# Row totals of the attention scores: accumulating DMAs in DRAM and a block transpose instead of products with a matrix of ones, for 21 of 32 graphs

## The chip, the core and the metric

The kernel runs on one core of one Trainium2 chip, in one launch. The metric is device time in microseconds (us); lower is better. A time is the median of several executions of the same program. Beside it stands one execution that was taken by the hardware profiler; all durations of single instructions come from that one.

The engines are called by their short names: PE is the matmul engine (PEld is its loading of weights), DVE the vector engine, ACT the scalar engine, POOL is GpSimd, SP the engine that issues most of the DMAs.

## What is computed

The input is `x`, 32 graphs of 512 nodes with 128 features each, and one 512 x 512 adjacency matrix `adj`. Four graph layers follow each other, each as `x = x + layer(relu(layernorm(x)))`. The change is in the first one:

```python
x_h = elu(x @ Wi + bi)
a_src = x_h @ We[:H, 0]
a_tgt = x_h @ We[H:, 0]
e = sigmoid(a_tgt[:, :, None] + a_src[:, None, :] + be[0])
e = e * (adj + ALPHA * (1.0 - (adj != 0)))
agg = einsum('bij,bjh->bih', e, x_h)
self_part = x_h * sum(e, axis=-1, keepdims=True)
recv = elu(concatenate([agg, self_part], -1) @ Wn + bn)
out = concatenate([recv, x_h], -1) @ Wm + bm
```

For each graph the scores `e` are a 512 x 512 matrix, and `self_part` needs the total of each of its 512 rows: these are the "score totals". Layer 2 (`layer1` in the code) is a gated recurrence of five steps with products by `adj`, layer 3 one product with `adj`, layer 4 a polynomial in `adj`.

## The kernel before, in words

**Layout.** Features (or source nodes) lie on the 128 partitions. One graph is a tile of 128 x 512 fp32 (256 KB), so nearly every instruction works on 128 x 512 elements. Scores are kept transposed, as four tiles `es[0..3]` (lines 701 to 710), one for each 128 source nodes, with all 512 target nodes along the free dimension. A total over the source nodes is therefore a sum over the four tiles and over the 128 partitions.

**The order of the work.** The kernel doesn't issue its instructions where they are written. Each step is listed with `op(engine, us, due, ...)`: an engine, an assumed duration, a due time, and what it reads and writes. A planner (`Plan`, lines 53 to 248) plays the program through with these assumed durations, and puts the steps of each engine in a fixed order. `slots` (line 301) gives the number of buffers of each kind, `ahead` how far it may look past the oldest step; `HEAD_NUDGES` (line 25) are seeds that shift some due times in the first 130 us of the plan. On the chip each engine runs its list in order, and waits by semaphores where a result is late. So a step that waits holds up everything that stands behind it on its engine, and for a DMA everything behind it in the queue of the engine that issues it. While nothing is ready for PE in the first 50 us of the plan, it issues small products of `ones` that nothing reads (`plan.idle`, line 347), here called fillers.

**A branch.** After some 11 us the kernel knows whether `adj` holds only zeros and ones (lines 586 to 596, 1106), and takes one of two arms. With these inputs it takes the binary one. In it, `adj` products run on PE in a one-pass format (fp32r), with the other operand split into a rounded part and a rest.

**Pipelining over graphs.** Graphs enter one after the other, some 50 us apart (`PACE`, `begin`, line 774), and several are in different layers at the same time. For a graph, `entry` and `scored` (line 625) make `xhT`, the messages `msg` and the score ends; `aggregated` (line 694) makes the scores, their products with the messages (line 715, bank `pn`), the totals, and the rest of the layer.

**The totals before.** For graphs 0 and 1 two DVE additions and two products with `ones`. For graph 2 three DVE additions, and for graphs 3 to 31 DMAs, add the four `es` tiles to one tile `sums` in SBUF: a copy issued by SP (line 740), then three accumulating DMAs issued by POOL (line 743), each of which waits for the one before it. The sum over the partitions is left to PE: ACT rounds `sums` to fp32r (line 747), DVE takes the rest (line 748), and two products with `ones_r` (line 753) add them up in a bank `ps`, where each total then stands on all partitions. DVE multiplies it with `xhT` (`own`, line 756), and the product of `own` with `Wn` is added to `pn` (line 758), which has stayed open until then.

**A column as a row.** `scored` already has a way to turn a column of four values per partition (the score ends) to a row on all partitions, without PE (lines 662 to 671): a DVE block transpose, a DMA to a small DRAM tile `d`, and a DMA that reads it back to all partitions.

**Layer norm.** Each layer norm (line 513) has DVE moments, a power on POOL (line 527) and a scaling on ACT (line 536). The powers share POOL's queue with the accumulating DMAs.

**Masks and loads at the start.** `adj` is loaded by ACT's queue (line 386), graphs and weights by SP's (lines 383 to 401). ACT copies `adj` to fp32r with its columns reordered (line 583, `nat`), copies its transpose (line 584, `adj_r`) and makes the four mask tiles (line 828). The products of line 906 make the square of `adj`.

Of the kernel before, what the change touches and what calls it, by code (L numbers as in the profile page):

```python
# [17 lines left out]
P = 128  # L18
# [6 lines left out]
HEAD_NUDGES = (7100000, 7100078, 7100153, 7100154, 7100740, 7100413, 7100768, 7100794, 7100559, 7100664, 7100595,  # L25
    7100631, 7100754, 7100963, 7100652, 7100659, 7100662, 7100678, 7100697, 7100699, 7100706,
    7100965, 7100730, 7100733, 7100742, 7100786, 7100966, 7100797, 7100813, 7100877, 7100824,
    7100834, 7100860, 7100864, 7100866, 7100875, 7100881, 7100884, 7100901, 7100907, 7100908,
    7100911, 7100919, 7100920, 7100922, 7100934, 7100936, 7100941, 7100945, 7100946, 7100949,
    7100950, 7100955, 7100970, 7100973)  # L30
# [22 lines left out]
class Plan:  # L53
# [74 lines left out]
    def known(self, o, to):  # L128

        own = {"PE": 0.0, "ACT": 0.13, "DVE": 0.13}  # L130
        if to.eng == o.eng in own:
            return o.known - o.result + own[o.eng]
        return o.known + (self.slack if to.eng == "PE" else 0.0)
# [118 lines left out]
def tile_four_graph_layers(  # L252
# [38 lines left out]
    FIRST = 4  # L291
    ONES = 0
    SPLIT = False
    SQUARE, NAT = 12.0, 0.0
    BRANCHES = 0.75
    A_LANDS = (3.0, 3.3, 3.6, 3.8)
# [4 lines left out]
    slots = {"x": 5, "f": 36, "q": 4, "s": 8, "d": 4, "m": 8, "b": 8}  # L301
    plan = Plan(slots, ahead=60.0, last=(B - 2) * PACE)
# [8 lines left out]
    def buffers(pool, kind, n, shape, dt=F32):  # L311
# [6 lines left out]
        "s": buffers(pool, "s", slots["s"], [P, 12 * NC]),  # L318
        "d": buffers(dram, "d", slots["d"], [P, 32]),
# [15 lines left out]

    def chunks(t):
        return t.rearrange("p (c d) -> p c d", c=NC)
# [4 lines left out]
    op("DVE", 0.2, -9, lambda: nc.vector.memset(at(ones), 1.0), [], [ones])  # L342
# [12 lines left out]
    op("ACT", 1.4, -9, lambda: nc.scalar.activation(  # L355
# [12 lines left out]
    def load_column(src, name, due, result=None):  # L368
        return load_const(src.rearrange("(p o) -> p o", o=1), [P, 1], name, due, 0.48, result=result)
# [7 lines left out]
    def load_graph(b, due, result=None):  # L377
        op("SP", 0.48, due, lambda: nc.sync.dma_start(
            at(X[b]), x[b].rearrange("(p c) d -> p c d", c=NC)),
            [], [X_group[b // G], X[b]] if b % G == 0 else [X[b]], result=result)  # L380


    load_graph(0, -10, 2.5)
    A_nat = [Val("f") for _ in range(NC)]
    for ic, v in enumerate(A_nat):
        load(v, adj.rearrange("(p c) n -> c p n", c=NC)[ic], -9.5, 0.45, result=A_LANDS[ic], eng="ACT")
    Wi_sb = load_const(Wi, [P, P], "Wi_sb", -9)
    bi_sb = load_column(bi, "bi_sb", -9)
    load_graph(1, -8.5, 4.3)
    load_graph(2, -8, 4.5)  # L390
# [3 lines left out]
    load(W_tok, Wn[:P], -7, to=lambda t: t[:, :P], result=4.5)  # L394
    load(W_tok, We.rearrange("(t p) o -> p (t o)", p=P), -7, to=lambda t: t[:, P:])
    be_sb = load_const(be.partition_broadcast(P), [P, 1], "be_sb", -7, result=4.3)
    Wn_sb = load_const(Wn[P:], [P, P], "Wn_sb", -6, result=4.0)
    bn_sb = load_column(bn, "bn_sb", -6, result=3.6)
    Wm_sb = load_const(Wm.rearrange("(t p) o -> p t o", p=P), [P, 2, P], "Wm_sb", -5)
    bm_bc = load_const(bm.partition_broadcast(P), [P, P], "bm_bc", -5, earliest=BRANCH)  # L400
    load_graph(3, -6, 3.6)
# [153 lines left out]
    plan.vals[mask] = True  # L555
# [22 lines left out]
    adj_r = const("adj_r", [P, NC, N], F32R)  # L578
    adj_rows = [Val(tile=adj_r.tile[:, jc, :]) for jc in range(NC)]
    plan.vals.update(dict.fromkeys([adj_r, *adj_rows]))  # L580
    nat = [Val("q") for _ in range(NC)]
    for jc, pt in enumerate(adjacency_turned(-1)):
        op("ACT", T_COPY, NAT + jc, lambda jc=jc: nc.scalar.copy(chunks(at(nat[jc])), by_token(A_nat[jc])), [A_nat[jc]], [nat[jc]])
        op("ACT", T_COPY, jc, lambda jc=jc, pt=pt: nc.scalar.copy(at(adj_rows[jc]), at(pt)),
           [pt], [adj_rows[jc], adj_r])
# [38 lines left out]

    def scored(b, hT, due):
# [33 lines left out]
        row, tgt = Val("d"), Val("f")  # L659

        flip = Val("s")
        def turn():
            nc.vector.transpose(
                at(flip)[:, :32].rearrange("p (k c) -> p k c", c=NC),
                at(ends)[:, None, NC : 2 * NC].to_broadcast([P, 32 // NC, NC]))
        def gather():
            nc.sync.dma_start(at(row), at(flip)[:, :32])
        def read():
            rows = at(row).rearrange("(q k) i -> q (k i)", k=32)[:, :P]
            nc.sync.dma_start(  # L670
                at(tgt).rearrange("p (q e) -> p q e", e=P), rows[None].to_broadcast([P, 4, P]))
# [12 lines left out]
        if b < G:  # L684
            tgt = Val("b")
            tgt.pieces = True
            op("PE", T_TR, d, spread, [ends, ident], [tgt])
        else:
            op("DVE", 0.1, d, turn, [ends], [flip])
            op("SP", T_DMA, d, gather, [flip], [row], result=2.6)  # L690
            op("SP", T_DMA, d, read, [row], [tgt], keep=KEEP, result=5.0)
        return xhT, msg, ends, tgt, like_tgt, of_tgt

    def aggregated(b, begun, due):
# [7 lines left out]
        for jc in range(NC):  # L702
# [5 lines left out]
                at(e), at(e), 1.0, at(mask)[:, jc, :], op0=ALU.add, op1=ALU.mult),  # L708
                [e, mask], [e], two=True)
            es.append(e)  # L710

        d = due + 30 * pace
        pn = Val("b")
        for jc in range(NC):
            op("PE", T_MM, d, lambda jc=jc: nc.tensor.matmul(  # L715
                at(pn), at(msg)[:, ts(jc, P)], at(es[jc]), start=jc == 0, stop=False),
                [msg, es[jc]], [pn])

        if b < ONES:
# [12 lines left out]
        else:  # L732
# [24 lines left out]
            at(own), at(xhT), at(ps), op=ALU.mult), [xhT, ps], [own])  # L757
        product(Wn_sb, own, d, pn, start=False)
# [59 lines left out]
    def list_rest(binary, pool):  # L818
        for v in crossing:
            v.left -= 1  # L820
        if binary:
            adjT, rows = adj_r, adj_rows
        else:
            adjT = Val(tile=pool.tile([P, NC, N], F32, tag="AT", name="AT"))
            rows = [Val(tile=adjT.tile[:, jc, :]) for jc in range(NC)]
        for jc, pt in enumerate([None] * NC if binary else adjacency_turned(9)):
            def masked(jc=jc):
                nc.scalar.activation(at(mask)[:, jc, :], at(adj_rows[jc]).bitcast(F32), AF.Identity,
                                     bias=at(ones)[:, :1], scale=1 / ALPHA - 1)
            if binary:  # L830
                op("ACT", T_COPY, 9 + jc, masked, [adj_rows[jc], ones], [mask])
                continue
            z, row = Val("f"), rows[jc]
            op("ACT", T_COPY, 9 + jc, lambda z=z, pt=pt: nc.scalar.mul(at(z), at(pt), 1 / ALPHA), [pt], [z])
            op("DVE", T_VEC, 9 + jc, lambda jc=jc, z=z, pt=pt: nc.vector.scalar_tensor_tensor(
                at(mask)[:, jc, :], at(pt), 0.0, at(z), op0=ALU.is_equal, op1=ALU.add),
                [pt, z], [mask])
            op("ACT", T_COPY, 9 + jc, lambda row=row, pt=pt: nc.scalar.copy(at(row), at(pt)),
               [pt], [row, adjT])
# [3 lines left out]
        n = 21 if binary else 16  # L843
# [57 lines left out]
        if binary:  # L901
            adj2T = Val(tile=pool.tile([P, NC, N], F32R, tag="AA", name="AA"))
            squares = [Val("b") for _ in range(NC)]
            for n in range(NC * NC):
                kc, jc = divmod(n, NC) if SPLIT else divmod(n, NC)[::-1]
                op("PE", T_PASS, SQUARE, lambda jc=jc, kc=kc, pt=squares[jc]: nc.tensor.matmul(  # L906
                    at(pt), at(nat[kc])[:, ts(jc, P)], at(rows[kc]), start=kc == 0, stop=kc == NC - 1),
                    [nat[kc], rows[kc]], [squares[jc]])
            for jc, pt in enumerate(squares):
                op("ACT", T_COPY, SQUARE, lambda jc=jc, pt=pt: nc.scalar.copy(  # L910
                    at(adj2T)[:, jc, :], at(pt)), [pt], [adj2T])
# [23 lines left out]
        adjQ = Val(tile=pool.tile([P, NC, N], R, tag="AQ", name="AQ"))  # L935
# [215 lines left out]
```

## Time and profile before

| | |
|---|---|
| median of 3 runs | 1607.69 us (1605.64 to 1608.5) |
| the profiled execution: its own time | 1605.48 us |
| its span, first to last instruction | 1603.6 us |
| granted PE clock | 1.00 |
| PE, records of matmuls | 6321 |
| DVE busy | 1404.7 us (88%) |
| ACT busy | 1130.4 us (70%) |
| POOL busy | 240.3 us (15%) |
| mean busy share of the DMA engines in 0 to 200 us, 200 to 1400 us | 10% to 76%, 45% to 47% |

How to read it. The span is what the profiler saw from the first to the last instruction; the execution's own time is 1.9 us longer. A busy time of PE is not yet proof that PE is at its limit, since the ends of matmuls are modelled. What shows it is the pace from start to start. An fp32 product with 512 columns leaves two records. The chain that ended last is followed back from the last instruction; a stretch of it on one engine with no wait of another engine in it means that this engine set the time there.

### The profile page before, as it was taken

The numbers are of one execution on the slowest core, as the hardware profiler recorded it, in microseconds if no ns is written. First come the engines' busy times: TensorE is split into PE (matmuls) and PEld (weight loads), VectorE is DVE, ScalarE is ACT, GpSimd is POOL, SyncE is SP. The second block draws the span as 40 slices with busy tenths as digits, with TensorE's granted clock in tenths as the row PEclk, the third lists the DMA queues.
The fourth block names the chain that finished last, engine by engine and source line by source line (L and its number), as shares of the span: only waits on it lengthen the run. The fifth ranks groups of instructions, "written<-read, shape, count | busy, mean of one in ns | idle before, by whom it ended". The sixth has DMA issues, their size and how long they took to land.

```text
span 1603.6 us, 20898 instructions
## 1 busy us (share of the span) xinstructions
PE 1596.1 (100%) x6321; PEld 1024.3 (64%) x6321; DVE 1404.7 (88%) x3314; ACT 1130.4 (70%) x2129; POOL 240.3 (15%) x240
## 2 busy tenths in 40 slices
PE   9999999999999999999999999999999999999998
PEld 7655555666666666666666666666666666656687
DVE  8899989998988899989988899888998889878862
ACT  8877777877866767667766678676787677665661
POOL 2121101211111111211111111111111101100010
PEclk9999999999999999999999999999999999999999
DMA  3365335443543345544445534454444444333221
GB/s 109 80 152 145 112 111 140 121 130 106 144 126 115 105 126 136 137 122 111 121 125 145 126 96 128 119 148 119 132 130 124 125 120 129 90 91 99 86 60 49
DMA packets 272634, 188.01 MB, mean 117 GB/s; under 512 B 77312, under 2 KB 221568, under 8 KB 272512
## 3 DMA queue, kind: packets, MB, share of 16 engines
q1 hardware_dynamic: 257824, 161.93, 33.8%
q0 software_dynamic: 12528, 22.81, 8.5%
q10 hardware_dynamic: 2160, 1.84, 0.3%
q8 instruction: 52, 0.85, 0.2%
q14 instruction: 70, 0.57, 0.1%
HBM read 82.78 MB, written 73.33 MB: 97 GB/s over the span
## 4 chain that ended last, share of the span: by engine, by line
PE 99%; DMA 0%; DVE 0%; ACTq 0%; issue 0%
PE b L490 46%; PE b L950 26%; PE b L1025 7%; PE b L715 7%; PE b L1034 4%; PE b L766 4%; PE b L643 2%; PE b L1013 2%; PE b L753 1%; DMA f<-in_adj_dram 0%; PE b L419 0%; PE b L347 0%; PE b L906 0%; ACTq L361 0%; PE b L680 0%; DVE s L522 0%
## 5 line engine op out<-in xcount | busy, mean ns | idle before, releaser
L479 ACT COPY f<-b 128x512 f32<-128x512 f32 x388 | 223.7, 584 | 146.5 <-PE b L950 101.1
L950 PE MATMUL b<-AQ,r 128*128 128x512 f32 x1024 | 305.4, 440 | 0.0
L527 POOL TENSOR_TENSOR s<-s,nhalf 128x4 f32<-128x4 f32 x128 | 156.6, 1231 | 968.2 <-DVE s L525 774.6
L950 PEld LDWEIGHTS b<-AQ,r 128*128 128x128 f32 x1024 | 192.3, 188 | 90.8 <-issue 50.0
L975 DVE TENSOR_TENSOR f<-f,b 128x512 f32<-128x512 f32 x320 | 212.7, 676 | 24.5 <-PE b L490 18.5
L431 DVE STREAM_TRANSPOSE f<-f 128x512 f32<-128x512 f32 x246 | 207.3, 846 | 20.7 <-ACT f L536 19.7
L536 ACT ACTIVATE f<-x,s 128x128 f32<-128x128 f32 x496 | 203.8, 487 | 27.7 <-DVE s L531 27.3
L950 PE MATMUL b<-adj_r,r 128*128 128x512 f32 x768 | 220.8, 430 | 0.0
L495 ACT ACTIVATE f<-f,b4w 128x512 f32<-128x512 f32 x160 | 115.6, 723 | 116.8 <-DVE f L975 116.3
L950 PEld LDWEIGHTS b<-adj_r,r 128*128 128x128 f32 x768 | 143.8, 188 | 59.2 <-issue 27.3
L924 DVE TENSOR_TENSOR r<-f,r 128x512 fp32r<-128x512 f32 x224 | 152.5, 683 | 13.1 <-ACT r L920 12.7
L490 PE MATMUL b<-f,w4T 128*128 128x512 f32 x320 | 163.2, 592 | 0.0
L490 PE MATMUL b<-f,u3T 128*128 128x512 f32 x320 | 163.1, 592 | 0.0
L490 PE MATMUL b<-f,w5T 128*128 128x512 f32 x320 | 162.9, 592 | 0.0
L490 PE MATMUL b<-f,u5T 128*128 128x512 f32 x320 | 162.9, 592 | 0.0
L490 PE MATMUL b<-f,w3T 128*128 128x512 f32 x320 | 162.7, 592 | 0.0
L495 ACT ACTIVATE f<-b,b5w 128x512 f32<-128x512 f32 x160 | 109.2, 684 | 54.9 <-PE b L490 49.9
L920 ACT CAST r<-f 128x512 fp32r<-128x512 f32 x224 | 137.7, 619 | 12.3 <-DMA f<-m 11.9
L495 ACT ACTIVATE f<-f,b3w 128x512 f32<-128x512 f32 x160 | 115.0, 721 | 38.9 <-DVE f L975 38.4
L992 DVE TENSOR_TENSOR f<-f,f 128x512 f32<-128x512 f32 x160 | 109.2, 683 | 30.7 <-ACT f L495 30.3
L1025 PEld LDWEIGHTS b<-V,f 128*128 128x128 f32 x1024 | 122.7, 192 | 14.8 <-issue 12.7
L743 POOL DMA_DIRECT2D f<-f x87 | 78.8, 918 | 348.9 <-DVE f L975 54.6
(114 smaller groups left out, 2370.4 us busy)
## 6 DMA issues: line engine op xcount, KB each, us to landing
m<-f SPq DMA_DIRECT2D x246, 256.0 KB, 2.1
f<-m SPq DMA_DIRECT2D x186, 256.0 KB, 2.9
f<-f POOLq DMA_DIRECT2D x87, 256.0 KB, 3.8
f<-m SPq DMA_DIRECT2D x240, 64.0 KB, 2.4
x<-in_x_dram SPq DMA_DIRECT2D x32, 256.0 KB, 3.1
f<-f SPq DMA_DIRECT2D x29, 256.0 KB, 2.4
f<-d SPq DMA_DIRECT2D x28, 256.0 KB, 5.5
out_dram<-x SPq DMA_DIRECT2D x28, 256.0 KB, 2.4
```

What stands on the lines that cost most here:

```text
L431: op("DVE", us, due, lambda: nc.vector.transpose(view_out(at(blocks)), view_in(at(src))), [src], [blocks])
L479: op("ACT", us, due, lambda: nc.scalar.copy(at(t), at(src)), [src], [t])
L490: nc.tensor.matmul(to, at(w), of, start=start, stop=stop)
L495: op("ACT", us, due, lambda: nc.scalar.activation(at(dst), at(src), AF.Tanh, bias=at(bias), scale=scale), [src, bias], [dst])
L527: op("POOL", 1.2, due, lambda: nc.gpsimd.tensor_tensor(stat(SCALE), stat(VAR), at(neg_half), op=ALU.pow), [s, neg_half], [s], two=False)
L536: nc.scalar.activation(at(h)[:, ts(c, P)], at(X[b])[:, c, :], AF.Relu, bias=stat(SHIFT)[:, c : c + 1], scale=stat(SCALE)[:, c : c + 1],)
L715: op("PE", T_MM, d, lambda jc=jc: nc.tensor.matmul(at(pn), at(msg)[:, ts(jc, P)], at(es[jc]), start=jc == 0, stop=False), [msg, es[jc]], [pn])
L920: op("ACT", T_COPY, due, lambda: nc.scalar.copy(part(hi), whole()), [src], [hi], keep=1)
L924: op("DVE", T_VEC, due, lambda: nc.vector.tensor_tensor(part(lo), whole(), part(hi).bitcast(F32), op=ALU.subtract), [src, hi], [lo], two=two)
L950: nc.tensor.matmul(at(pa), at(part)[:, ts(jc, P)], view(at(columns)[:, jc, :]), start=jc == n == 0, stop=jc == NC - 1 and n == PARTS - 1,)
L975: op("DVE", T_VEC, d, lambda: nc.vector.tensor_tensor(at(s), at(u), at(pg), op=ALU.add), [u, pg], [s])
L1025: nc.tensor.matmul(at(pz)[:, ts(i, D)], at(t[i])[:, ts(ic, P)], at(V[k]), start=i == n == 0, stop=last and i == G - 1 and n == len(terms) - 1,
```

## The change

Five things are changed.

1. **Totals of graphs 7 to 27** (`FIRST_TREE`, `TREES`): 21 graphs. The four `es` tiles are added in a DRAM tile `half` (kind `m`, as used by the transposes) instead of an SBUF tile; then a fourth accumulating DMA adds the lower 64 rows of it to the upper 64 (DRAM to DRAM). SP loads 32 of these 64 rows as a 128 x 128 tile `few`, and a fifth accumulating DMA adds the other 32. DVE transposes `few` in blocks of 32 x 32 and reduces 32 values each to one: four totals per partition. The way of the score ends, now a function `as_row`, puts them as a row on all partitions of an SBUF tile. The fp32r split and the two products with `ones_r` are gone for these graphs. Since that takes longer, the rest of the layer is due 52 us later (`TREE`), and the bank `pn` doesn't stay open over that time: ACT copies it to SBUF, and later back to a bank, to which the product with `Wn` is added.
2. **Masks**: the four mask tiles are made by POOL instead of ACT, in the binary arm.
3. **Loads**: graph 1 is issued ahead of `Wi`, graph 3 directly after graph 2, the small columns behind them; the planner is given other landing times for them.
4. **The square of `adj`**: `nat` is copied in its order in memory, and the products read its columns with a stride; `mask`, `adj_r` and others are tracked by rows.
5. **The plan**: more buffers of kinds `s`, `d`, `m` and a kind `y`; `ahead` is 110 instead of 60; `SQUARE` is 9 instead of 12; other seeds in `HEAD_NUDGES`; a due time in the middle graphs is 2.2 instead of 2.0 `PACE`.

The core of the diff:

```diff
+    FIRST_TREE, TREES, TREE = 7, 28, 52
-    SQUARE, NAT = 12.0, 0.0
+    SQUARE, NAT = 9.0, 0.0
-    slots = {"x": 5, "f": 36, "q": 4, "s": 8, "d": 4, "m": 8, "b": 8}
-    plan = Plan(slots, ahead=60.0, last=(B - 2) * PACE)
+    slots = {"x": 5, "f": 36, "q": 4, "s": 10, "d": 6, "y": 3, "m": 10, "b": 8}
+    plan = Plan(slots, ahead=110.0, last=(B - 2) * PACE)
...
-    Wi_sb = load_const(Wi, [P, P], "Wi_sb", -9)
-    bi_sb = load_column(bi, "bi_sb", -9)
-    load_graph(1, -8.5, 4.3)
-    load_graph(2, -8, 4.5)
+    load_graph(1, -8.5, 2.9, 3.0)
+    Wi_sb = load_const(Wi, [P, P], "Wi_sb", -8.2, earliest=3.0, result=2.7)
+    load_graph(2, -8, 2.9, 3.0)
+    load_graph(3, -7.5, 3.1, 3.0)
+    bi_sb = load_column(bi, "bi_sb", -7.2, earliest=4.0, result=2.5)
...
-        op("ACT", T_COPY, NAT + jc, lambda jc=jc: nc.scalar.copy(chunks(at(nat[jc])), by_token(A_nat[jc])), [A_nat[jc]], [nat[jc]])
+        op("ACT", T_COPY, NAT + jc, lambda jc=jc: nc.scalar.copy(at(nat[jc]), at(A_nat[jc])), [A_nat[jc]], [nat[jc]])
...
+    def totals(es, d):
+
+        half, few, turned_few, columns = Val("m"), Val("y"), Val("y"), Val("s")
+        def strip(k):
+            return at(half)[ts(k, 32), :].rearrange("j (q i) -> q j i", q=4)
+        def added(to, of, val):
+            op("POOL", 1.0, d, lambda: nc.gpsimd.dma_start(to(), of(), accum_op=ALU.add),
+               [*val, val[-1]], [val[-1]], two=False, result=4.6)
+        op("SP", T_DMA, d, lambda: nc.sync.dma_start(at(half), at(es[0])), [es[0]], [half], result=2.6)
+        for e in es[1:]:
+            added(lambda: at(half), lambda e=e: at(e), [e, half])
+        added(lambda: at(half)[: P // 2, :], lambda: at(half)[P // 2 :, :], [half])
+        op("SP", T_DMA, d, lambda: nc.sync.dma_start(at(few), strip(0)), [half], [few], result=2.6)
+        added(lambda: at(few), lambda: strip(1), [half, few])
+        op("DVE", 0.25, d, lambda: nc.vector.transpose(at(turned_few), at(few)), [few], [turned_few])
+        op("DVE", 0.25, d, lambda: nc.vector.tensor_reduce(
+            at(columns)[:, :NC], at(turned_few).rearrange("p (b j) -> p b j", j=32),
+            axis=mybir.AxisListType.X, op=ALU.add), [turned_few], [columns])
+        return columns
...
-        if b < ONES:
+        if tree:
+            columns, part = totals(es, due + 22), copied(pn, d)
+            due += TREE
+            d += TREE
+            ps = as_row(columns, lambda t: t[:, :NC], d - 6, 2)
+        elif b < ONES:
...
         own = Val("f")
         op("DVE", T_VEC, d, lambda: nc.vector.tensor_tensor(
-            at(own), at(xhT), at(ps), op=ALU.mult), [xhT, ps], [own])
-        product(Wn_sb, own, d, pn, start=False)
+            at(own), at(xhT), at(ps), op=ALU.mult), [xhT, ps], [own], two=tree)
+        if tree:
+            pn = Val("b")
+            pn.added = True
+            op("ACT", T_COPY, d, lambda: nc.scalar.copy(at(pn), at(part)), [part, own], [pn])
+        op("PE", T_MM, d, lambda: nc.tensor.matmul(
+            at(pn), at(Wn_sb), at(own), start=False, stop=True, skip_group_check=tree), [own, Wn_sb], [pn])
...
-                nc.scalar.activation(at(mask)[:, jc, :], at(adj_rows[jc]).bitcast(F32), AF.Identity,
-                                     bias=at(ones)[:, :1], scale=1 / ALPHA - 1)
+                nc.gpsimd.tensor_scalar(at(mask[jc]), at(adj_r[jc]).bitcast(F32), 1 / ALPHA - 1, 1.0,
+                                        op0=ALU.mult, op1=ALU.add)
...
-                    at(pt), at(nat[kc])[:, ts(jc, P)], at(rows[kc]), start=kc == 0, stop=kc == NC - 1),
+                    at(pt), by_token(nat[kc])[:, jc, :], at(adjT[kc]), start=kc == 0, stop=kc == NC - 1),
```

Counted in the two programs, in the arm that runs: the products of `ones_r` go from 60 to 18, the fillers from 34 to 37, and every other product keeps its count. DVE loses 21 subtractions and gains 21 transposes of 128 x 128, 21 reductions and 21 of the small transposes. ACT loses 21 roundings and 4 masks, and gains 42 copies of 128 x 512. POOL's accumulating DMAs go from 87 to 129. SP issues 63 DMAs more.

## The prediction

> **What bounds the kernel.** I read the page first, then the chain of waits in a stretch of the steady state and at the end, then the busy times by stretch, then the groups and the DMA issues.
>
> The page's busy times, and its chain that ended last (share of the span by engine, then by line; b is any PSUM bank):
>
> ```profile
> PE 1596.1 (100%) x6321; PEld 1024.3 (64%) x6321; DVE 1404.7 (88%) x3314; ACT 1130.4 (70%) x2129; POOL 240.3 (15%) x240
> ...
> PE 99%; DMA 0%; DVE 0%; ACTq 0%; issue 0%
> ```
>
> The whole chain is PE. But is PE at its own pace there, or are waits hidden in its busy time? Two rows of PE's timeline (start, duration, instruction): the first ends at 732.93, after the second has started, so the durations overlap and are no measure.
>
> ```profile
> 731.91 1.02 PE L490 MATMUL b<-f,Wi_sb 128*128 128x512 f32 x2
> 732.37 1.03 PE L753 MATMUL b<-q,ones_r 128*128 128x512 f32 x2
> ```
>
> The chain counts from one to the next. Its pieces in the same place (start us, us, what):
>
> ```profile
> 732.07 0.86 PE b L490 x2
> 732.93 0.47 PE b L753 x2
> 733.39 4.29 PE b L490 x10
> ...
> 739.44 1.85 PE b L950 x8
> 741.28 1.78 PE b L766 x16
> ```
>
> An fp32 product (two records) takes 0.86 us whether alone or five in a row (4.29 / 5); a one-pass product 1.85 / 8 = 0.231; a 128-wide fp32 one 1.78 / 8 = 0.223. These paces are the same in every stretch. At them, 868 wide fp32 products (1736 records of line 490) come to 745 us, 2048 one-pass products with `adj` or its square to 474, 1024 narrow ones (2048 records of lines 1025, 766, 643, 1013) to 229, 128 score products of line 715 to 110, 60 of line 753 to 14, and the rest (transposes, fillers, making the square) to some 22: 1594 us. PE starts at 1.0 and ends at 1598.5 us. So some 3.5 us of PE's time is waiting, in a span of 1603.6.
>
> Where are they? Busy times by stretch (us of the stretch, then PE, PEld, DVE, ACT, POOL busy with instructions; clock, DMA share, GB/s):
>
> ```profile
> 0.00:20.00 20.00, 17.77 (x109) 15.25 (x110) 13.22 (x59) 16.32 (x28) 6.45 (x18) 1.00 0.64 189
> 20.00:40.00 20.00, 19.80 (x106) 13.58 (x106) 19.79 (x60) 17.91 (x40) 4.48 (x5) 1.00 0.10 31
> 40.00:60.00 20.00, 20.00 (x88) 12.62 (x87) 18.75 (x48) 18.43 (x38) 3.76 (x3) 1.00 0.14 46
> ...
> 600.00:800.00 200.00, 200.00 (x796) 128.69 (x796) 181.61 (x434) 143.96 (x277) 30.74 (x29) 1.00 0.46 125
> ```
> All of PE's idle time is in the first 40 us (2.2 + 0.2). From 40 us on it is full. So each microsecond of work taken from PE after that comes off the end, if nothing else becomes late; the last stage after PE (a DVE addition of 0.69 us and the last store) is untouched.
>
> [...] The rows from start to start decide here: the loads hide behind products of 0.43 us a record, and the products follow each other without a gap. I take the full value.
>
> **Totals: what goes from PE.** 21 graphs x 2 products of line 753 = 42, at 0.47 / 2 = 0.234 us: 9.8 us, all of it after 140 us, where PE is full. Nothing is added to PE: the product with `Wn` and the four score products stay. The 3 fillers more (34 to 37) fill idle time by their nature: 3 x 0.224 = 0.7 us if that were wrong.
>
> **DVE.** 21 subtractions go, at 0.682 (the group of line 748: 20.5 us for 30). Per graph come a small transpose (0.20, line 663), a transpose of 128 x 128 and a reduction of 128 x 128. For these two: above, 0.28 each (line 859, 128 x 128 addition, 0.283); below, 0.20 (the 128 x 32 transpose); I take 0.26. Sum 0.72 - 0.68 = +0.04 x 21 = +0.8 us on 1404.7. DVE stays at 88%: no cost; its ends are 0.60 to 0.76.
>
> **ACT.** 21 roundings at 0.616 go (12.9), 42 copies at 0.584 to 0.598 come (24.8), 4 masks at 0.714 go (2.7), the four `nat` copies drop from 1.149 to about 0.6 (a plain copy; -2.2): +7 us, 1137 of 1594, 71%. What hides it is ACT's idle 470 us; with that cover gone 7 us would be the price. The copy back to a bank stands directly ahead of the `Wn` product, but needs only `own`, so it adds 0.6 us to the graph's chain, not to PE.
>
> **The chain of the totals, and who stands behind it.** The accumulating DMA is the step whose place is new. Rows of before (KB, us from issue to landing):
>
> ```profile
> m<-f SPq DMA_DIRECT2D x246, 256.0 KB, 2.1
> f<-m SPq DMA_DIRECT2D x186, 256.0 KB, 2.9
> f<-f POOLq DMA_DIRECT2D x87, 256.0 KB, 3.8
> ...
> f<-f SPq DMA_DIRECT2D x29, 256.0 KB, 2.4
> f<-d SPq DMA_DIRECT2D x28, 256.0 KB, 5.5
> ```
> No row shows an accumulation in DRAM. The nearest is the one in SBUF, 3.8 (3.3 to 5.6 over the 87). A plain write to DRAM is 0.3 quicker than one to SBUF (2.1 against 2.4), a plain read of it 0.5 slower (2.9 against 2.4), and the accumulation does both: 3.8 + 0.2 = 4.0 is my value. Ends: 3.5 (it gains from the write alone) and 5.6 (the slowest of before). [...] I stay with 4.0, and keep 5.6 for the rival. A link of the chain is the landing and some 0.45 to the next issue (line 743 was issued at 518.82, 523.09 and 527.18 us: 4.2 apart).
>
> Before: store 2.6, 3 links of 4.25, rounding 0.6, subtraction 0.7, products 0.5, `own` 0.7: 17.9 us. After: store 2.6, 5 links of 4.45, load of `few` 3.4, three DVE steps 0.8, store to `d` 1.9, read 6.0, `own` 0.7, copy 0.6: 38.3 us. So it is 20.4 us longer. What covers it: in the two orders of PE's instructions, the work between a graph's last score product and its `Wn` product is 21.7 us (median) before, and 45.5 for the 21 graphs after (43.4 to 51.6), at the paces above. That is 23.8 more. The old chain already had a margin: in four graphs between 500 and 700 us the last accumulation landed 1.0, 4.6, 2.6 and 3.9 us before the rounding began, 3.0 in the mean. Margin after: 3.0 + 23.8 - 20.4 = 6.4 us, or 1.3 for each of the five links. So the totals are not late, by my value; they cost nothing on PE.
>
> Behind the accumulating DMAs on POOL stand the powers of layer norms (line 527), and behind the loads of `few` and of the row on SP the stores and loads of the transposes. POOL's idle time ended by DMAs of that line was 35.5 us over the whole span, without a stall on PE after 40 us. 42 more issues at 0.918 are 39 us on an engine that is 15% busy. The planner assumes 5.6 us a link, above the 4.45 that I expect, so what stands behind each is placed late enough. DMA engines: 0.5 MB more per graph is 11 of 188 MB; their share goes from 46% to about 49%.
>
> **Masks, loads, the square.** All of this lies before 40 us, where PE has 2.4 us of idle time and 11.2 us of fillers: 13.6 us that aren't work. Before the branch little can move: the chain starts with the last part of `adj`, landing at 7.8 us, with the DMA engines full (358 to 397 GB/s from 6 to 8 us). Graph 1 goes ahead of `Wi`, but SP's queue had moved both by then, so the total in front of `adj` is about the same: 0, with ends -0.4 and +0.7 (one 256 KB transfer at 360 GB/s). Four masks on POOL: the nearest row, a 128 x 128 cast at 0.29, gives 0.9 for 512 columns, 3.6 us between two layer norm powers, so graph 1's normalisation is later by some 0.6 to 1 us and graph 2's by up to 2.7; ACT, full from 11 to 25 us, loses 2.7 there and about 2 before the branch. The two pull in opposite directions; the program places 19 fillers after the branch instead of 17. I take 0 for the head, with ends -2 and +2.5.
>
> **The sum.** 1605.5 (the profiled execution) - 9.8 + 0 = 1595.7, span 1593.8. The median of the runs is 2.2 above that execution: 1607.7 - 9.8 = 1597.9.
>
> **The rivals.**
> - *Full value and a better head* (4%): the ACT time freed in the head shortens the fillers by over 3 us: 1594.5 or less. Against it: the order has more fillers, not fewer.
> - *Part is given back* (18%): some of the 21 graphs come to the `Wn` product late, in stretches where the DMA engines are at 76%, or DVE at 96% (100 to 200 us); or the head loses over 2 us. At 0.2 us a graph, 4.2 us: 1602. For it: the margin of 6.4 is a mean, and 1.0 was seen before; against: from 40 us on no stall was seen at all. A third of it falls within 0.2% of no change.
> - *Accumulating in DRAM is slow* (10%): one mechanism, the link. From a landing of 4.0 + 1.3 + 0.1 = 5.4 us the wait (0.47 us a graph) eats the gain. At the slowest landing seen, 5.6, it is 5 x 1.6 - 6.4 = 1.6 us a graph, PE waiting at `Wn` with all products behind it: 34 - 9.8 = +24, 1632 us. For it: no row shows this form, and DRAM is read and written in one. Against: both plain rows.
> - *PE isn't the bound* (in the second's chance): then 1607.7, no change; the start-to-start rows exclude most of it.
>
> **How the numbers follow.** Likeliest, full value with the head at -2 to +2.5: 68%, 1595.5 to 1600.5. The range takes that, the first rival's near end and most of the second: 1594 to 1604.5. A measurement can tell 0.2%, 3.2 us, from no change: faster is below 1604.5. Faster 0.68 + 0.04 + 0.11 = 0.83; same 0.07; slower 0.10.
>
> **What would show it.** Right: line 753's group at 18 records, PE still full in every stretch after 40 us, the chain 99% PE, the same paces; accumulations into `m` landing at 3.5 to 4.5 us; POOL's powers not waiting longer. Wrong: PE idle time, or weight loads waiting for `own` ahead of the `Wn` product, or landings above 5.4 us; fillers plus idle time in the head far from 13.6 us.

## The result, and the profile after

The changed kernel takes 1611.51 us (median of 22 runs, 1607.16 to 1618.27), the kernel before 1606.54 (22 runs beside it). The ratio is 1.0031, with a 95% interval of 1.0022 to 1.0040: slower by 5 us, where 1597.9 was forecast. The profiled execution of the changed kernel took 1614.92 us, span 1613.1, some 3 above its median.

The page after: the busy times, two DMA queues (packets, MB, share of 16 engines), and the chain that ended last.

```profile
PE 1594.4 (99%) x6285; PEld 1017.6 (63%) x6285; DVE 1407.0 (87%) x3356; ACT 1134.0 (70%) x2146; POOL 282.5 (18%) x286
...
q1 hardware_dynamic: 274708, 169.16, 35.2%
q0 software_dynamic: 24288, 27.01, 12.3%
...
PE 31%; DVE 0%; issue 0%
```

PE has 36 records fewer (42 products of `ones_r` gone, 6 records more of fillers), as the change says. Line 784, the old 753, is down to 18. But the chain is PE for 31% only: followed back from the end it breaks off at 1108 us, where PE waited for something. In the kernel before it was PE for 99%. The busy times by stretch show the same (us of the stretch, then PE, PEld, DVE, ACT, POOL busy; clock, DMA share, GB/s):

```profile
200.00:400.00 200.00, 197.92 (x712) 120.96 (x711) 184.84 (x455) 148.88 (x285) 38.26 (x35) 0.99 0.51 131
...
600.00:800.00 200.00, 197.04 (x765) 124.19 (x764) 177.98 (x424) 143.39 (x270) 38.06 (x36) 1.00 0.54 131
800.00:1000.00 200.00, 196.58 (x765) 123.80 (x764) 177.60 (x423) 141.64 (x270) 37.58 (x36) 1.00 0.54 136
...
1200.00:1400.00 200.00, 199.97 (x757) 124.58 (x756) 174.24 (x381) 138.71 (x259) 28.53 (x28) 1.00 0.48 122
```

Before, the stretch of 600 to 800 had 200.00 of 200 and a DMA share of 0.46. Now PE loses 1.4 to 3.4 us in each stretch in which the 21 graphs are at work (1.8 from 400 to 600 us, 1.4 from 1000 to 1200, not shown), and next to nothing behind them.

To see how much time that costs, all of PE's records are taken at the prediction's paces from start to start (0.429, 0.231 and 0.112 us); what is over counts as waiting, with the stretches of halved clock in it (see the last section). In the two profiled executions:

| us | before | after | difference |
|---|---|---|---|
| work at those paces | 1585.6 | 1575.8 | -9.8 |
| fillers, start to start | 10.4 | 12.1 | +1.7 |
| waiting in 0 to 150 us | 2.1 | 1.8 | -0.3 |
| waiting in 150 to 1250 us | -0.3 | 17.4 | +17.7 |
| waiting after 1250 us | -0.7 | -0.1 | +0.6 |

The 9.8 us were gained, exactly as summed. 17.7 us of waiting came in, all in the stretch of the 21 graphs; so the question is what PE waits for there. (This execution is 3.4 us above the median of the changed kernel, so at the median some 14 is a fair estimate.)

**One stall, followed back.** The largest single wait after 340 us is at 803 us. PE's timeline (start, duration, instruction, idle time before it and who ended it):

```profile
801.49 1.88 PE L741 MATMUL b<-f,f 128*128 128x512 f32 x4
805.60 1.13 PE L793 MATMUL b<-f,Wn_sb 128*128 128x512 f32 x2 [2.24 <-ACT b L792]
```

It is the `Wn` product of a graph with the new totals, and it waits for ACT's copy back to the bank. Is the total late? DVE's product with the total (`own`) and ACT's timeline answer:

```profile
800.99 0.69 DVE L787 TENSOR_TENSOR f<-f,f 128x512 f32<-128x512 f32 x1
...
802.83 0.62 ACT L955 CAST r<-f 128x512 fp32r<-128x512 f32 x1 [3.01 <-DMA f<-m]
803.35 0.72 ACT L501 ACTIVATE f<-f,b4w 128x512 f32<-128x512 f32 x1
803.98 0.56 ACT L485 COPY f<-b 128x512 f32<-128x512 f32 x1
804.44 0.59 ACT L508 COPY b<-l2b 128x512 f32<-128x512 f32 x1
804.96 0.59 ACT L792 COPY b<-f 128x512 f32<-128x512 f32 x1
```

No: `own` was done at 801.68 us, before PE stopped at 803.4. The copy stands fifth in this piece of ACT's list, behind a rounding of line 955, of another layer, that waited 3.01 us for a transpose's tile (`f<-m`). And why was that late? SP's issues in order:

```profile
789.96 1.72 SPq L640 DMA_DIRECT2D f<-d  x2
791.96 0.33 SPq L439 DMA_DIRECT2D m<-f  x1
799.65 0.36 SPq L450 DMA_DIRECT2D f<-m  x1
```

Two row reads (`f<-d`: a 2 KB row of DRAM to all 128 partitions) went out at 789.96 and 791.31, then the store of the transpose. That store landed 7.6 us after its issue, against a median of 2.4, and only then could the read be issued. By the trace's list of packets, the 1024 packets (512 bytes each) of the two row reads moved between 791.5 and 798.4 us, and the 128 packets of the store behind them in the same queue only from 797.0 to 799.2. The DMA engines were half to four fifths free meanwhile (the last two numbers are their share and GB/s):

```profile
792.00:794.00 2.00, 2.00 (x9) 1.49 (x8) 2.00 (x4) 1.88 (x5) 0.00 (x0) 1.00 0.49 91
794.00:796.00 2.00, 2.00 (x6) 0.95 (x5) 0.38 (x2) 1.73 (x5) 0.00 (x0) 1.00 0.21 61
796.00:798.00 2.00, 2.00 (x6) 0.86 (x5) 1.62 (x2) 2.00 (x6) 0.00 (x0) 1.00 0.38 128
```

So it wasn't the totals that were late: a transfer of another layer, which had been just in time, got slow, and each of the lists of ACT and PE has one fixed order.

The waits of ACT for DMAs (total us, times, longest), after:

```profile
ACT r L955 <- DMA f<-m: 38.1, 29, 4.4
ACT f L729 <- DMA f<-d: 10.5, 8, 2.6
```

and before:

```profile
ACT r L920 <- DMA f<-m: 11.9, 13, 1.8
ACT f L704 <- DMA f<-d: 5.2, 5, 2.3
```

Both kinds of waiting have grown, the reads of transposes threefold. Line 729 makes scores from the row of the score ends, so it is the old `as_row`, not the totals' one. The other stalls of 0.8 us and more, read the same way: three go back to `f<-m` (535, 549, 996 us), three to `f<-d` (652, 706, 1102 us), and one (332 us, 2.24) to DVE's block transpose of line 659, which waited 3.3 us for the fifth accumulation. The root of the one at 1107 us (0.94) is open.

Three of these stalls (652, 803, 996 us) reach PE through the copy back to the bank, which the kernel before doesn't have. In the group of these products, the last numbers are PE's idle time and what ended it:

```profile
L793 PE MATMUL b<-f,Wn_sb 128*128 128x512 f32 x64 | 33.1, 599 | 4.7 <-ACT b L792 4.7
```

That is 4.7 of the 11.7 us for which PE is idle in the middle. No kernel without this copy was run, so what it adds isn't shown.

The landings after (KB, median us; the trace tells all those of POOL, but of SP's only 35 of the 267 stores and 2 of the 49 row reads):

```profile
m<-f SPq DMA_DIRECT2D x267, 256.0 KB, 2.4
f<-m SPq DMA_DIRECT2D x186, 256.0 KB, 3.0
m<-f POOLq DMA_DIRECT2D x63, 256.0 KB, 4.3
...
f<-d SPq DMA_DIRECT2D x49, 256.0 KB, 5.6
...
m<-m POOLq DMA_DIRECT2D x21, 128.0 KB, 3.3
...
y<-m POOLq DMA_DIRECT2D x21, 64.0 KB, 4.7
```

The five accumulations of a graph take 3 x 4.3 + 3.3 + 4.7 = 20.9 us, where 5 x 4.0 = 20 was forecast. The rival that called accumulation in DRAM slow is out. For SP's transfers these medians are too thin to say by how much they became slower.

### The profile page after: what moved, and what is told of

It reads as the page before. It is cut to its first block, busy times and chain, and to the rows that moved or that the text cites. A ratio compares the mean times of both kernels' runs of the same rounds, so it can differ in the third digit from the quotient of the medians.

```text
span 1613.1 us, 21201 instructions
## 1 busy us (share of the span) xinstructions
PE 1594.4 (99%) x6285; PEld 1017.6 (63%) x6285; DVE 1407.0 (87%) x3356; ACT 1134.0 (70%) x2146; POOL 282.5 (18%) x286
## 3 DMA queue, kind: packets, MB, share of 16 engines
q1 hardware_dynamic: 274708, 169.16, 35.2%
q0 software_dynamic: 24288, 27.01, 12.3%
## 5 line engine op out<-in xcount | busy, mean ns | idle before, releaser
L485 ACT COPY f<-b 128x512 f32<-128x512 f32 x409 | 234.8, 584 | 157.8 <-PE b L985 109.1
L985 PE MATMUL b<-adj_r,r 128*128 128x512 f32 x768 | 225.4, 436 | 0.0
L955 ACT CAST r<-f 128x512 fp32r<-128x512 f32 x224 | 137.2, 619 | 42.3 <-DMA f<-m 38.1
L1060 PE MATMUL b<-V,f 128*128 128x128 f32 x1024 | 123.7, 275 | 0.0
```

What stands on the lines that cost most here:

```text
L485: op("ACT", us, due, lambda: nc.scalar.copy(at(t), at(src)), [src], [t])
L955: op("ACT", T_COPY, due, lambda: nc.scalar.copy(part(hi), whole()), [src], [hi], keep=1)
L985: nc.tensor.matmul(at(pa), at(part)[:, ts(jc, P)], view(at(columns[jc])), start=jc == n == 0, stop=jc == NC - 1 and n == PARTS - 1,)
L1060: nc.tensor.matmul(at(pz)[:, ts(i, D)], at(t[i])[:, ts(ic, P)], at(V[k]), start=i == n == 0, stop=last and i == G - 1 and n == len(terms) - 1,
```

## The experiments

Theory A: the second row read of a graph holds up the transposes' DMAs and the score rows. Rival B: DVE's wait for the fifth accumulation (line 659) holds up what stands behind it. Rival C: the new settings of the plan, not the totals. Rival D: the accumulating DMAs' own traffic. First four kernels that were planned anew or changed in one place; then cuts that keep the order of every engine.

**e1: the changed kernel without its totals.**

```diff
-    FIRST_TREE, TREES, TREE = 7, 28, 52
+    FIRST_TREE, TREES, TREE = 7, 7, 52
```

> The changed kernel with the totals of all graphs made as before (SBUF sums, products of ones); masks, loads and plan settings stay changed. If the new totals cause the loss (by the row reads, by the DVE wait or by the accumulating traffic): PE full again after 40 us, no waits over 1 us there, and only the head's difference left, about +1.5 us: 1608. If the new plan settings (ahead 110, other due times, more buffers) are the cause: the waits of 10 to 17 us stay and the 9.8 us of PE work come back: 1616 to 1621.

Measured: 1613.03, ratio to before 1.0032 (1.0019 to 1.0045). In the middle PE is full, with the records of before:

```profile
150.00:1250.00 1100.00, 1100.00 (x4206) 693.86 (x4205) 1000.12 (x2344) 790.70 (x1503) 165.11 (x155) 1.00 0.46 125
```

So the waits in the middle go with the totals. This order is a new one too, so e1 alone can't tell the totals from the order; g1 below, which keeps the changed kernel's order, can. What makes e1 slower lies elsewhere. In its profiled execution, which is 9.1 us above that of before, it is 1.5 in fillers, 1.5 of waiting in the head, 1.0 from 40 to 150 us, and 5.1 after 1250 us (one wait of 2.3 us, and a halved clock behind it; the mean granted clock of the execution is 0.998). Waits from 40 to 150 us and after 1250 us are not in the changed kernel, so they belong to this order and not to the change. Fillers are the part of rival C that both share.

**e2: the totals' row read issued by POOL instead of SP.**

```diff
-            ps = as_row(columns, lambda t: t[:, :NC], d - 6, 2)
+            ps = as_row(columns, lambda t: t[:, :NC], d - 6, 2, "POOL")
```

> The changed kernel with one thing different: the read of the totals' row (256 KB from the small DRAM tile, 21 times) is issued by POOL instead of SP. Theory A (the second row read per graph holds up the transposes' stores and loads and the score rows behind it in SP's DMA queue): most of the ends in waits for transposes and score rows go, 5 to 9 us less: 1603 to 1606. Theory B (DVE stands at the block transpose until the fifth accumulation has landed, with gates of other graphs behind it): no change, 1611, plus or minus 2. Theory D (the accumulating DMAs themselves slow all other transfers): no change, 1611.

Measured: 1614.55, ratio 1.0040 (1.0025 to 1.0055); 13.9 us of waiting in the middle. Nothing is gained. That doesn't clear SP's queue, though: the planner gave this kernel another order on PE, ACT and DVE, the read now stands ahead of the accumulating DMAs in POOL's queue, and it lands no sooner there (5.5 us in the median, all 21).

**e3: the kernel before with a second read of the score row for 21 graphs.** Its order is that of before; the second row goes to a DRAM tile that nobody reads.

```diff
+            if 7 <= b < 28:
+                nc.sync.dma_start(
+                    again[b % 2].rearrange("p (q e) -> p q e", e=P), rows[None].to_broadcast([P, 4, P]))
```

> The kernel before, with every instruction in its place, and for graphs 7 to 27 a second read of the score row issued by SP directly behind the first, to a DRAM tile that nothing reads. Theory A: 3 to 8 us longer than before (1610 to 1614), with waits for transposes and score rows on ACT, and then on PE, as in the changed kernel. Theories B and D: as before, 1606.5, within 1 us, since neither the DVE wait nor an accumulation is added.

Measured: 1644.52, ratio 1.0242 (1.0225 to 1.0258): 36.6 us above before for 21 reads of 256 KB, 1.74 us each, and 35.9 us of waiting in the middle. Its waits of ACT are those of the changed kernel, only more:

```profile
ACT r L924 <- DMA f<-m: 48.2, 27, 4.5
ACT f L708 <- DMA f<-d: 12.5, 10, 2.9
```

A row read that nobody waits for is enough to make PE wait. Here it is issued directly behind another one, which the changed kernel does only at times, and it also writes its 256 KB to DRAM, which no read of the changed kernel does. So the size doesn't carry over, and that it is the reading and not the writing which costs is left to f4, g2 and g4.

**e4: the planner told that the fifth accumulation lands later (9.0 instead of 4.6).**

> The changed kernel, where the planner is told that the fifth accumulating DMA lands after 9.0 us instead of 4.6, so that the DVE transpose of it stands later in DVE's order. Theory B: DVE no longer waits for that landing, 2 to 4 us less: 1607.5 to 1609.5. Theory A: the rows are read as before, so the waits for transposes and score rows stay: 1611, plus or minus 2.

Measured: 1635.73, ratio 1.0176 (1.0159 to 1.0193), 31.8 us of waiting in the middle. The number moves the whole order, and the new order is worse. It doesn't tell A from B. What follows is only that two orders of the same work differ by 24 us, so the next cuts had to keep the order.

**f1: the totals' row read a quarter as long.**

```diff
+            if total is not None:
+                nc.sync.dma_start(at(t)[:, :P], rows[0][None].to_broadcast([P, P]))
+                return
```

> The changed kernel, every instruction of every engine in its place; the read of the totals' row moves a quarter of it (64 KB instead of 256 KB; the rest of the tile keeps old values, so the totals are left out for three of four node groups). Theory A (the 21 reads of one 2 KB row by all partitions hold up the transposes and the score rows that are in flight beside them): PE's waits after 150 us, 17 us in the changed kernel's profile, fall to 5 or less: 1598 to 1602. Theory B (DVE waits for the fifth accumulation): 1609 to 1611.5. Theory D (the accumulating DMAs): 1609 to 1611.5.

Measured: 1604.31, ratio 0.9984 (0.9977 to 0.9990): 7.2 us less than the changed kernel. ACT's waits for score rows (`f<-d`) fall from 10.5 us to 1.4; those for transposes (`f<-m`) stay:

```profile
ACT r L958 <- DMA f<-m: 35.8, 31, 4.0
ACT f L732 <- DMA f<-d: 1.4, 2, 0.9
```

**f2: no wait of DVE for the accumulations.**

```diff
-        op("DVE", 0.25, d, lambda: nc.vector.transpose(at(turned_few), at(few)), [few], [turned_few])
+        op("DVE", 0.25, d, lambda: nc.vector.transpose(at(turned_few), at(ident)), [few], [turned_few])
```

> The changed kernel, every instruction in its place; the DVE block transpose of the totals reads a constant tile instead of the accumulated one, so that DVE doesn't wait for the fifth accumulation (the totals come out as constants; all DMAs are issued as before). Theory B: PE's waits fall to 5 us or less: 1598 to 1602. Theory A: only the one wait of 2.2 us that starts at this transpose goes, with what follows from it: 1607 to 1610. Theory D: no change, 1611.

Measured: 1611.28, ratio 1.0028 (1.0019 to 1.0036): as the changed kernel. DVE's 12.2 us of waiting at line 659 are gone, and the time stays. Rival B falls, although the stall at 332 us begins there.

**f3: the 105 accumulating DMAs not issued.**

```diff
-            op("POOL", 1.0, d, lambda: nc.gpsimd.dma_start(to(), of(), accum_op=ALU.add),
+            op("POOL", 1.0, d, lambda: None,
```

> The changed kernel, every other instruction in its place, without the 105 accumulating DMAs of the 21 graphs (the totals are of one quarter of the nodes only). Theory D (their traffic slows all else): PE's waits fall to 5 us or less: 1598 to 1602. Theory A: as with the DVE wait taken away alone, 1606 to 1610, since the rows are read as before. Theory B: 1598 to 1602 too, since nothing is left that DVE could wait for.

Measured: 1606.50, ratio 1.0001 (0.9993 to 1.0009): 5.0 us less than the changed kernel. Here it is ACT's waits for `f<-m` that fall most, from 38.1 us to 20.3:

```profile
ACT r L955 <- DMA f<-m: 20.3, 17, 3.5
ACT f L729 <- DMA f<-d: 5.8, 7, 2.7
```

Rival D holds too, for some 5 us. The DMAs also take time on POOL (busy for 206.7 us from 150 to 1250 us in the changed kernel, for 111.1 here), where the powers of the layer norms stand behind them; but DVE's waits for these powers are 8.5 us in the changed kernel and 8.3 here, so POOL's time isn't what is given back.

**f4: as many bytes, but not one row.** The totals' row read is replaced by a read of 256 KB of `x`, 512 pieces from 512 places, each to one place.

```diff
+                nc.sync.dma_start(
+                    at(t).rearrange("p (q e) -> p q e", e=P), x[total].rearrange("(q p) e -> p q e", p=P))
```

> The changed kernel, every instruction in its place; the read of the totals' row moves the same 256 KB in pieces of the same 512 B, but from 512 different places (a graph's input) instead of one 2 KB row read by all partitions, and doesn't wait for the small tile (the totals are replaced by input values). Theory A, if it is the one row that is slow: most of the gain of the quarter read, 1599 to 1604. Theory A, if it is the number of pieces: no change, 1611. Theories B and D: no change, 1609 to 1611.5.

Measured: 1605.29, ratio 0.9990 (0.9983 to 0.9996): 6.2 us less than the changed kernel, with the same bytes and the same size of packets. It also has no wait for the small tile ahead of the read; g4 and g2 below are free of that.

**g1: f1 and f3 together.**

> The changed kernel with both of the earlier cuts at once: the totals' row read brings a quarter of its bytes, and the 105 accumulating DMAs of the totals aren't issued; the order on every engine is kept. It leaves out the sums of the totals and three quarters of their rows. One cut gave 1604.3, the other 1606.5, from some 1611.3. If the two loads each add their own delay (theory: row reads and additions both, some 6 us each), this comes to 1598 to 1601, a ratio of .995 to .997, and 3 us or less of waiting on PE after 150 us. If either alone already brings the traffic below a point where something just late becomes on time (a threshold), the second cut adds nothing: 1603 to 1606.

Measured: 1597.86, ratio 0.9948 (0.9934 to 0.9961). One cut gave 7.2 us, the other 5.0, both together 13.7: they add up, and a threshold, by which either cut alone would have been enough, is excluded. PE is full again in the middle:

```profile
150.00:1250.00 1100.00, 1099.90 (x4208) 692.22 (x4207) 1008.85 (x2418) 811.49 (x1538) 113.23 (x96) 1.00 0.39 114
```

against the changed kernel's

```profile
150.00:1250.00 1100.00, 1088.31 (x4128) 679.61 (x4127) 991.10 (x2369) 796.76 (x1512) 206.68 (x195) 1.00 0.53 134
```

80 records more in the same 1100 us, in the same order of PE. ACT's waits are back where they were before the change: 12.9 us for `f<-m`, 0.4 for `f<-d`. The time is also what the prediction's sum gives when the two loads that it lacked are taken away: -9.8 us on PE and +1.2 in fillers make -8.6, and 8.7 us were gained on the runs.

**g2 and g4: every row read as four DMAs of 32 partitions.** The small DRAM tile holds eight equal copies of the row, each in four pieces of 512 bytes (the block transpose writes 32 columns for 4 values). In g2 each of the four DMAs reads another copy, in g4 all read the first. All 49 reads are made so; nothing is left out.

```diff
-            rows = at(row).rearrange("(q k) i -> q (k i)", k=32)[:, :P]
-            nc.sync.dma_start(
-                at(t).rearrange("p (q e) -> p q e", e=P), rows[None].to_broadcast([P, 4, P]))
+            rows = at(row).rearrange("(q k) i -> q (k i)", k=32)
+            for g in range(4):
+                nc.sync.dma_start(
+                    at(t)[ts(g, 32), :].rearrange("p (q e) -> p q e", e=P),
+                    rows[:, ts(g, P)][None].to_broadcast([32, 4, P]))
```

In g4 the last line has `ts(0, P)`.

> The changed kernel, with each row read (49, the score ends' and the totals') made by four DMAs of 32 partitions, each of which reads another one of the eight equal copies that the small DRAM tile holds. Nothing is left out. If the single 2 KB row, read by 128 partitions, is what makes these reads slow and harmful (theory: one place in DRAM), four places give a part of what 512 places gave: landings below 4.5 instead of 5.6, and 1604 to 1609. If the number of descriptors or their size does it (rival), it stays at 1610 to 1614.

> The control: the changed kernel with the row reads made by four DMAs of 32 partitions, which all read the same copy. Nothing is left out. By the theory of one place in DRAM: landings as in the changed kernel (5.5 or more), 1610 to 1615, and slower than the kernel with four copies. By the rival (the split into four DMAs is what matters): as the kernel with four copies.

Measured: g2 1603.32, ratio 0.9982 (0.9973 to 0.9991); g4 1612.89, ratio 1.0035 (1.0021 to 1.0049). The middle stretch of g2:

```profile
150.00:1250.00 1100.00, 1098.16 (x4194) 689.23 (x4194) 1006.25 (x2414) 807.01 (x1530) 211.87 (x201) 1.00 0.54 136
```

and of g4:

```profile
150.00:1250.00 1100.00, 1090.94 (x4142) 682.33 (x4141) 995.02 (x2373) 800.10 (x1517) 206.27 (x195) 1.00 0.54 135
```

The two have the same number of DMAs, the same bytes, the same share of the DMA engines (0.54), and differ by 9.6 us. Only the places in DRAM that are read differ. Their landings (45 of the 196 are told), g2:

```profile
f<-d SPq DMA_DIRECT2D x196, 64.0 KB, 2.4
```

and g4:

```profile
f<-d SPq DMA_DIRECT2D x196, 64.0 KB, 3.5
```

In g2 ACT never waits for `f<-d` any more, in g4 it waits 6.1 us in total. g2 is the fastest kernel of the study that leaves nothing out: 8.2 us ahead of the changed kernel, 3.2 ahead of the one before.

**g3: the kernel before with four copies.**

> The kernel before with the same four reads from four copies for its 28 row reads. Nothing is left out. PE hardly waits there, so by either theory the time stays within 0.1% of 1606.5; a gain larger than that would mean that even 28 row reads cost PE time. Landings of the row reads: below 4.5 by the theory of one place, 5.5 by the rival.

Measured: 1606.09, ratio 0.9996 (0.9988 to 1.0005): no change, though the landings fall from 5.5 (one DMA) to 2.4 (each of four), with all of them told in both traces:

```profile
f<-d SPq DMA_DIRECT2D x112, 64.0 KB, 2.4
```

In the kernel before PE doesn't wait for the 28 reads, so their price isn't seen in the time. It is seen in the landings of others, and these two kernels show it most cleanly, since every engine keeps its order. 26 transfers are issued by SP as the first or second behind a row read and within 3 us of it. Their median landing is 5.0 us in the kernel before and 3.0 with four copies, and each of the 26 is quicker; the 732 that come over 8 us behind a row read land in 2.6 in both. That is the trap: what a read does to others cost nothing, until 21 more came.

## Why the prediction was wrong

- **PE is the bound, a microsecond of its work is worth one**: right. Work fell by 9.8 us, and g1 shows the gain when nothing else comes in (-8.7). In the kernel before PEld is busy for 64% of the span, while PE is 99% of the chain that ended last.
- **DVE and ACT hidden**: right. DVE +2.3 us (forecast +0.8), ACT +3.6 (forecast +7).
- **The chain of the totals, 20.4 us longer, with a margin of 6.4**: landings near the forecast (20.9 against 20; one into DRAM took 4.3, one into SBUF 3.7 in the same kernel, so accumulating in DRAM was the slower by 0.6 us, where the prediction had put 0.2 on the SBUF landing of before, but it stayed well under the 5.4 us that the rival needed). The mean margin hid that some come late: DVE waited 7 times for `few`, up to 3.5 us. But f2 shows that those waits are worth nothing in the end.
- **The head at 0**: off by a little. Fillers are 12.1 us instead of 10.4 in the profiled execution, 11.4 to 12.4 in the experiments made from the changed kernel.
- **What failed**: the steps "what stands behind each is placed late enough" and "DMA engines: [...] their share goes from 46% to about 49%". The first asked only for the queues, and was answered by the planner's assumption of 5.6 us a link; in fact SP's queue stood at the row reads for 35.2 us in 23 waits for the small tile's store, against 10.5 us in 11 before (f1 still has 25.0 us of this and gains 7.2, so it isn't the main price). The second counted bytes, and took a mean share below one as free. Both put at nothing what a transfer costs the other transfers under way. The share came to 0.53: the accumulating DMAs held the engines longer than their bytes say (by the page q0 goes from 8.5% to 12.3% for 4.2 MB more; before, q1 moved 162 MB in 33.8%). By the runs this is some 5 us (f3). And a row read by all partitions delayed what was issued behind it, at a share of 0.46 from 150 to 1250 us (before: landings of 5.0 us instead of 2.6) as at 0.53 (after): 6 to 8 us (f1, f4, and g2, which changes the 28 older reads too). The sum of the prediction lacked these two terms, 13.7 us by g1. A smaller step failed with them: that the copy back "needs only `own`" and adds nothing to PE. It also stands in ACT's list, behind whatever waits there, and 4.7 us of PE's idle time end with it.
- **The rivals**: "part is given back" came nearest, with `Wn` products that come late. But it had them late by the totals' own chain; the transposes (`f<-m`) and score rows (`f<-d`), which have less margin, were not looked at. Its 4.2 us would have been 13.7.

What stays open: why one DRAM row read by many is slow inside the memory, since no run shows more than that the place decides; whether transfers of another queue are delayed by it as well; how the accumulations' 5 us divide between DMA engines and DRAM; what the copy back to the bank adds; and what the 3.3 us of waiting are that g2 still has in the middle.

## What to carry to other kernels

Where the bound engine is full and its list has a fixed order, a new transfer is priced, as here (13.7 us by g1, against 9.8 us of work saved), by what it does to the transfers that are already just in time: look up the waits for each DMA that are short now, and how many, and ask which of them the new one is beside. A share of the DMA engines doesn't tell it: at 0.54, PE waited 14.6 us in the profile of one kernel (g4) and 3.3 in that of another (g2). The landings do: in the trace of before, transfers right behind a row read already took 5.0 us instead of 2.6. Spread a small DRAM operand that many partitions read over several copies, if they are there anyway, before adding more such reads: with four copies instead of one the same DMAs landed in 2.4 us instead of 3.5, and the kernel took 1603.32 us instead of 1612.89 (g2, g4).

## What was not expected of the hardware

**One row for all.** In the kernel before, 256 KB read from one 2 KB row of DRAM land in 5.5 us (28 reads), 256 KB from 512 places in 2.9 (`f<-m`, 186 reads). Four DMAs of a quarter each land in 3.5 us from one copy (g4), in 2.4 from four (g2, g3).

**A halved clock after a short wait.** In the changed kernel's profiled execution the granted clock was 0.5 for 3.41 us, from 336.29 to 339.70 us, behind the stall at 332 us (busy times and clock as above):

```profile
332.00:334.00 2.00, 0.92 (x3) 0.09 (x1) 1.33 (x4) 0.00 (x0) 0.00 (x0) 1.00 0.09 28
334.00:336.00 2.00, 1.00 (x3) 0.53 (x4) 2.00 (x4) 0.72 (x1) 0.00 (x0) 1.00 0.72 229
336.00:338.00 2.00, 2.00 (x5) 1.05 (x4) 2.00 (x6) 1.69 (x4) 0.00 (x0) 0.57 0.83 151
338.00:340.00 2.00, 2.00 (x6) 1.57 (x6) 2.00 (x6) 1.76 (x4) 0.00 (x0) 0.57 0.22 33
```

PE was idle for 2.08 us there by its timeline. The stretch at half the clock costs another 1.7, an estimate from its 3.41 us at 0.5; PE counts as busy in it. From 340 us to PE's last instruction the clock stayed at 1.00, though PE was idle for 2.24 us at 803 us, longer than at 332. The profiled execution of e3, with waits of 1.98 and 2.64 us among others, had a mean granted clock of 0.996, that of f2, with waits of 2.15 and 2.94, one of 0.998; before it was 1.000. What makes the clock fall after one wait and not after another is not shown.
